# Layer 2's first norms and part products inside layer 1's last pair, and one pool for masked weights and parts

## The chip, the cores and the metric

The kernel runs on one core of one Trainium2 chip. The metric is the device time of one execution in microseconds (us); lower is better. A core has five engines that matter here: TensorE (PE), which multiplies matrices; VectorE (DVE); ScalarE (ACT); GpSimd (POOL); and SyncE (SP), which in this kernel only issues transfers. POOL issues transfers as well. Weights of a matmul are loaded into PE by an instruction of their own (PEld in the profile).

## The reference, cut to what matters

Four graph layers run one after another on `x` of shape (8, 2048, 64). Each adds its result to its input: normalise the 64 features, clip at zero, apply the layer, add. The change touches the seam between layer 1 and layer 2.

```python
# layer 1: attention over the neighbours
h = maximum(layernorm(x), 0)
h1 = h @ W
e = leaky_relu(s_src[:, :, None] + s_dst[:, None, :], 0.2)
attention = softmax(where(adj > 0.5, e, NEG_INF), axis=2)
x = x + elu(attention @ h1)

# layer 2: three steps of message passing, then layer 3
v = maximum(layernorm(x), 0)
v[:, 0] = intervention_value
for _ in range(3):
    effects = adj @ v
    h = relu(concat([v, effects]) @ W1.T + b1)
    v = h @ W2.T + b2
x = x + v
# layer 3: x, A x and 2 A (A x) - x, each with its own weights per node
```

## The kernel before, in words

The batch of 8 is handled as four pairs (`NP`). The two members of a pair lie one above the other in the 128 partitions, features by nodes, so a pair is a tile of 128 x 2048. It is worked on in four chunks of 512 nodes (`NCW`, `CW`). The adjacency stays on chip as sixteen tiles of 128 x 2048 (`aT` 0 to 11 and `aTl` for the last four).

**Layer 1** (`Layer1`, `run` at L1410) goes through the pairs. For a pair, `attend` (L1350) works on each half of the nodes: for each of sixteen tiles `m`, DVE makes two masked-weight tiles `pt` of 128 x 1024 (L1379), PE multiplies them with the features `hS` into `o` (`features`) and with `vd` into the denominator `dn` (`sums`). The order of the two alternates from tile to tile, so that the profile shows them as groups of two tiles. After each tile's first product, `between(m)` lets other work into the stream: the ends of the half before (`total`, whose product is `prd`, and `end`, which makes `res` and `e` and adds `e` to the pair's `x1` in memory by a POOL transfer), and a step of `neighbour_steps` (L1284). Those steps prepare the next pair: load `x`, norm it (`norm_steps`: `mean`, `xc`, square, `var`, logarithm and exponential, product), multiply with the weights (`ph`), and write the attention's row values to memory, from which `R` is loaded, one row repeated in all partitions. In the last pair there is no next pair and `between` only handles the ends.

**Layers 2 and 3** (`layers23`, L1474) begin when layer 1's pools are closed. `enter` (L1573) takes each chunk of the first pair through `normed` (L1542: the same norm) and `moved` (L1516): four products `py` with `W1e`, which are split into a high and a low part, `hi` by ACT (L1527) and `lo` by DVE (L1528). PE multiplies both parts with the adjacency, 16 tiles x 2 parts of 512 columns into `acc`. The first two chunks' input goes into `f_in`'s buffers, the other two into `room`, which shares its memory with the later `y1`. After the four `enter` chains the weights of layer 3 (`W3f`, `embf`) are loaded and two DVE operations (L1616, L1617) form combinations of them. Then come, for each pair, three steps of layer 2 and the products of layer 3. During the first two steps of each pair, raw adjacency chunks are loaded (`raw`, L1491) and checked on DVE (`check`, L1501).

The order of work on PE in both stages is that of the program (`kit.strict`, and `mm` at L713, whose line most matmuls carry). On the other engines a scheduler orders the instructions when the kernel is built. `Weave` interleaves the chains of layers 2 and 3 by the written delays. All pools have `reuse_waits="tile"`: a tile that takes over memory waits for the last user of the tile that lay there. Layer 1's pools are `l1_sb` and `l1_R` (right end of the on-chip memory), `att_pt` with 5 buffers for `pt`, and `att_sb`; layer 2 and 3 have `f_in`, `w2f` and `f_sb`, with 6 buffers each for `hi` and `lo`.

Of the kernel before, what the change touches and what calls it, by code (L numbers as in the profile page):

```python
# [16 lines left out]
P = 128  # L17
# [4 lines left out]
CW = 512  # L22
# [599 lines left out]
class Kit:  # L622
# [88 lines left out]
    def mm(self, *args, **kw):  # L711

        one = self.nc.tensor.matmul(*args, **kw)  # L713
        if self.strict:
            self.tc.keep_in_program_order(one)
# [10 lines left out]
    def norm_steps(self, dst, src, mean, var, xc, q):  # L726

        nc, mm = self.nc, self.mm
        n = dst.shape[-1] // CW
        for c in range(n):  # L730
            mm(mean[:, cols(c)], self.avg, src[:, cols(c)], start=True, stop=True)
        nc.vector.tensor_sub(xc, src, mean)
        nc.scalar.activation(q, xc, AF.Square)
        yield
        for c in range(n):
            mm(var[:, cols(c)], self.avg, q[:, cols(c)], start=True, stop=True)
        nc.scalar.activation(q, var, AF.Ln, bias=self.eps)
        nc.scalar.activation(q, q, AF.Exp, scale=-0.5)
        nc.vector.scalar_tensor_tensor(dst, xc, 0.0, q, op0=OP.max, op1=OP.mult)
        yield  # L740
# [525 lines left out]
class Layer1:  # L1266
# [6 lines left out]
    def __init__(self, kit, x1_dram):  # L1273
        tc, nc, t = kit.tc, kit.nc, kit.t
        self.kit, self.x1_dram = kit, x1_dram
        self.turn = 0
        self.l1 = l1 = ExitStack()
        dram = l1.enter_context(tc.tile_pool(name="r_dram", bufs=1, space=DRAM))
        self.r_dram = dram.tile([NP, 2, N], FP, name="r_dram")
        self.sb = sb = l1.enter_context(tc.tile_pool(name="l1_sb", bufs=2, side="right", reuse_waits="tile"))  # L1280
        self.R = l1.enter_context(tc.tile_pool(name="l1_R", bufs=2, side="right", reuse_waits="tile"))
        self.ps = ps = l1.enter_context(tc.tile_pool(name="l1_ps", bufs=1, space=PSUM, reuse_waits="tile"))

    def neighbour_steps(self, p):  # L1284

# [1 line left out]
        kit, sb, ps, Wx = self.kit, self.sb, self.ps, self.kit.W1x  # L1287
        nc, mm = kit.nc, kit.mm
        x1_dram, r_dram = self.x1_dram, self.r_dram
        hS = (self.sb2 if p % 2 else sb).tile([P, NT, P], FP, tag="hS", name="hS", bufs=1)  # L1290
        vd = sb.tile([P, NT, 2], FP, tag="vd", name="vd")
        sc = sb.tile([P, NT, 4], FP, tag="sc", name="sc", bufs=1)
        wd = sb.tile([P, NT, 2], FP, tag="wd", name="wd")
        for c in range(NCW):
            x = sb.tile([P, CW], FP, tag="x", name="x1", bufs=1)
            nc.sync.dma_start(out=x, in_=x1_dram[p, :, cols(c)])
            mean = ps.tile([P, CW], FP, tag="ln", name="mean")
            var = ps.tile([P, CW], FP, tag="ln", name="var")
            xc = sb.tile([P, CW], FP, tag="xc", name="xc")
            q = sb.tile([P, CW], FP, tag="q", name="q", bufs=1)  # L1300
            hn = xc
            for _ in kit.norm_steps(hn, x, mean, var, xc, q):
                yield
            for g in range(2):
                if g:
# [13 lines left out]
            yield  # L1319
# [30 lines left out]
    def attend(self, aT, p, hS, vd, wd, hf, between):  # L1350
# [24 lines left out]
        for m in range(NT):  # L1375
# [8 lines left out]
            order[0](m, pts)  # L1384
            between(m)
            order[1](m, pts)
        ds = self.sb.tile([P, CW], FP, tag="xc", name="ds")
        nc.vector.tensor_scalar_max(ds, dn, 1e-30)
        den = sb.tile([P, HN], FP, tag="den", name="den", bufs=1)

# [16 lines left out]

        return [lambda: total(0), end]

    def run(self, aT, now):  # L1410


        kit, l1 = self.kit, self.l1
        tc, nc = kit.tc, kit.nc
        self.pt = l1.enter_context(tc.tile_pool(name="att_pt", bufs=5, reuse_waits="tile"))
        self.sb2 = sb = l1.enter_context(tc.tile_pool(name="att_sb", bufs=2, reuse_waits="tile"))
        self.ps2 = l1.enter_context(tc.tile_pool(name="att_ps", bufs=2, space=PSUM, reuse_waits="tile"))
        kit.use_ln_exp()
        kit.strict = True
        ends = []  # L1420
        for p in range(NP):
            steps = self.neighbour_steps(p + 1) if p + 1 < NP else iter(())
            after = []

            def between(m):
                if m % NT and ends:
                    ends.pop(0)()

                for _ in range((2, 0, 1, 0, 1)[m % 5] - (m % 20 == 0)):
                    after.append(next(steps, None))  # L1430

            for hf in range(2):
                ends = self.attend(aT, p, *now, hf, lambda m: between(hf * NT + m))
            after.extend(steps)
            now = next((r for r in after if r), None)
        for e in ends:
            e()
        kit.strict = False
        l1.close()

# [30 lines left out]
            self.step(c)  # L1471


def layers23(kit, aT, x2_dram, x3_dram, out):  # L1474

    tc, nc, t, mm = kit.tc, kit.nc, kit.t, kit.mm
    ctx = ExitStack()
    W1v, W1e, W2, Wvc, Wec, cb = kit.W1v, kit.W1e, kit.W2, kit.Wvc, kit.Wec, kit.cb
    b1, b2c, ivc, b1c = kit.b1, kit.b2c, kit.ivc, kit.b1c
    K3, D3 = 3, 16  # L1480
    LAST = NCW - 1

    fin = ctx.enter_context(tc.tile_pool(name="f_in", bufs=2, reuse_waits="tile"))
    w2 = ctx.enter_context(tc.tile_pool(name="w2f", bufs=1, reuse_waits="tile"))
    sb = ctx.enter_context(tc.tile_pool(name="f_sb", bufs=2, reuse_waits="tile"))
    ps = ctx.enter_context(tc.tile_pool(name="f_ps", bufs=2, space=PSUM, reuse_waits="tile"))
    weave = Weave()
    todo = [(m, h) for m in range(NT) for h in range(NCW)]
    v = fin.tile([P, N], FP, name="v", bufs=1)

    def raw(n):  # L1491

# [15 lines left out]

    def parts(lent):

        tags = (lent, lent) if lent else (("hi", 6), ("lo", 6))
        return [sb.tile([P, 4, P], FR, tag=g, name=n, bufs=k) for n, (g, k) in zip(("hi", "lo"), tags)]

    LENT = (None, None, ("fold", 2), ("pr", 3))

    def moved(v, c, W, bias, lent=None):  # L1516

        py = ps.tile([P, 4, P], FP, tag="tp", name="py")
        for k in range(4):
            m = 4 * c + k  # L1520
            mm(py[:, k, :], v[:, m * P : (m + 1) * P], W, start=True, stop=True)
        hi, lo = parts(lent)
        if bias is not None:
            yb = fin.tile([P, 4, P], FP, tag="ca", name="yb")
            nc.vector.tensor_tensor(yb, py, bias[:, None, :].to_broadcast([P, 4, P]), op=OP.add)  # L1525
            py = yb
        nc.scalar.copy(hi, py)  # L1527
        nc.vector.tensor_tensor(lo, py, hi.bitcast(FP), op=OP.subtract)  # L1528
        return hi, lo
# [40 lines left out]
    def chunk_of(src, c):  # L1570
        return load(fin.tile([P, CW], FP, tag="x", name="xp"), src, c)
# [29 lines left out]
        yn[c] = turned(y1, c)  # L1601

    kit.strict = True
    y = [None] * NCW
    room = sb.tile([P, N], FP, tag="y1", name="room", bufs=1)
    for c in range(NCW):
        xp = chunk_of(x2_dram[0], c) if c < 2 else load(room[:, cols(c)], x2_dram[0], c)
        weave.start(enter(c, y, xp, 2.0 * c, ("u0", "u1")))
    weave.until(lambda: not weave.chains)
    W3 = w2.tile([P, K3, D3 * F], FP, name="W3f")  # L1610
    for h in range(2):
        nc.sync.dma_start(out=W3[half(h)], in_=t["L3_gnn_weight"])
    emb = w2.tile([P, NT, D3], FP, name="embf")
    nc.sync.dma_start(out=emb, in_=t["L3_gnn_embedding"].rearrange("(t p) d -> p t d", p=P))

    nc.vector.tensor_sub(W3[:, 0, :], W3[:, 0, :], W3[:, 2, :])  # L1616
    nc.vector.tensor_scalar(W3[:, 2, :], W3[:, 2, :], 2.0, None, op0=OP.mult)  # L1617
    every = range(NT)
    for p in range(NP):
        for step in range(3):  # L1620
            yn = [None] * NCW
            for c in range(NCW):
                acc = ps.tile([P, CW], FP, tag="acc", name="acc")
                if step < 2:
# [89 lines left out]
def four_layers(  # L1714
# [13 lines left out]
    with ExitStack() as s:  # L1728
# [29 lines left out]
            return steps()  # L1758

        layer0(kit, hn, x1, early, late_tile, between)  # L1760
        ahead[0].run(aT, ahead[1])
        layers23(kit, aT, x1, x3, out)
        ps = s.enter_context(tc.tile_pool(name="flag_ps", bufs=1, space=PSUM))
        nc.vector.tensor_reduce(kit.bad[:, 0:1], kit.bad, AX.X, OP.add)
        pb = ps.tile([F, 1], FP, name="pbad")
# [46 lines left out]
```

## Time and profile before

| | us |
|---|---|
| median of 3 runs | 2111.59 (2110.44 to 2114.61) |
| the profiled execution | 2106.54 |
| its span, first to last instruction | 2104.7 |
| layer 1's first attention product | starts at 529.08 |
| layer 1's last attention product | ends at 938.98 |
| first `acc` product of layer 2 | starts at 970.56 |
| granted TensorE clock, mean | 0.983 |

A line of a group gives the line of the program, the engine, the operation, what is written and what is read, the shapes and the count. In the chain and in the lists in order of time, the first number is the start in us from the span's beginning and the second the length. A product of fp32 operands is recorded as two instructions. "issue" is time for which the profile shows no cause. The span is cut into windows where that is more telling than the whole.

### The profile page before, as it was taken

To read this page: it belongs to the slowest core of one execution; us is meant where nothing else is said; L and a number is where in the kernel's file an instruction comes from. 1 tells how busy PE (TensorE), PEld (TensorE's weight loads), DVE (VectorE), ACT (ScalarE), POOL (GpSimd) and SP (SyncE) were. 2 spreads that over 40 slices of the span, in tenths; PEclk is the share of its full clock that TensorE was granted. 3 is DMA by queue.
4 is the path that set the end of the run, shared out by engine and by line. 5 is a ranking of instruction groups with operands and counts; after the bars stand their busy time and mean duration, and the time that the engine had idled before them with its cause. 6 is when DMAs were issued, how large, how long until landed. Compare 5 with 4: busy or idle time off the path is not lost.

```text
span 2104.7 us, 23660 instructions
## 1 busy us (share of the span) xinstructions
PE 2018.4 (96%) x9164; PEld 1156.8 (55%) x9164; DVE 1212.0 (58%) x1906; ACT 461.8 (22%) x863; POOL 260.1 (12%) x384
## 2 busy tenths in 40 slices
PE   7999989978999999997999999999999999999997
PEld 4777655623223233225776557775477755577653
DVE  6676488867888989973224662216542246522355
ACT  4322144466112121012121111110111211112100
POOL 0211154411000000000001120002110012100022
PEclk9999899989999999998999999999999999999999
DMA  5666271154111111113210012201012001121000
GB/s 128 195 187 192 100 233 47 36 160 155 51 46 36 41 40 31 41 23 91 66 45 14 23 32 60 63 10 30 23 54 66 30 21 25 37 65 55 5 16 12
DMA packets 85001, 136.06 MB, mean 65 GB/s; under 512 B 32912, under 2 KB 33168, under 8 KB 82640
## 3 DMA queue, kind: packets, MB, share of 16 engines
q1 hardware_dynamic: 66832, 83.86, 13.6%
q0 software_dynamic: 18048, 50.60, 8.9%
q8 instruction: 74, 1.21, 0.2%
q14 instruction: 47, 0.39, 0.1%
HBM read 103.69 MB, written 30.74 MB: 64 GB/s over the span
## 4 chain that ended last, share of the span: by engine, by line
PE 67%; issue 15%; DVE 6%; POOL 5%; DMA 3%; ACT 2%; POOLq 0%; SPq 0%; DVEq 0%; ACTq 0%
PE acc L713 27%; PE o L713 11%; PE dn L713 6%; PE u L713 5%; PE acc L925 2%; PE pgs L1153 2%; PE var L713 2%; PE py L713 2%; PE mean L713 2%; POOL fold L1699 1%; DVE ex L1151 1%; POOL ot L1700 1%; PE ph L713 1%; POOL mix L1152 1%; DMA at<-in_adjT 1%
## 5 line engine op out<-in xcount | busy, mean ns | idle before, releaser
L713 PE MATMUL acc<-aT,hi 128*128 128x512 f32 x960 | 419.7, 437 | 0.0
L713 PE MATMUL acc<-aT,lo 128*128 128x512 f32 x960 | 379.6, 395 | 0.0
L1687 DVE TENSOR_TENSOR pr<-u,embf 128x512 f32<-128x512 f32 x256 | 170.7, 688 | 138.8 <-PE u L713 131.8
L1379 DVE SCALAR_TENSOR_TENSOR pt<-R,wd,aT 128x1024 f32<-128x1024 f32 x192 | 236.9, 1280 | 22.2 <-PE dn L713 9.4
L713 PE MATMUL o<-pt,hS 128*64 128x512 f32 x1024 | 238.9, 602 | 4.1 <-DVE pt L1379 4.1
L713 PE MATMUL u<-W3f,y 64*128 64x512 f32 x1024 | 241.0, 589 | 0.0
L713 PEld LDWEIGHTS acc<-aT,hi 128*128 128x128 f32 x960 | 180.6, 188 | 66.0 <-issue 29.2
L713 PEld LDWEIGHTS acc<-aT,lo 128*128 128x128 f32 x960 | 180.7, 188 | 56.8 <-issue 20.1
L713 PEld LDWEIGHTS u<-W3f,y 64*128 64x128 f32 x1024 | 99.2, 187 | 120.6 <-issue 120.6
L713 PEld LDWEIGHTS o<-pt,hS 128*64 128x64 f32 x1024 | 70.4, 137 | 164.0 <-issue 149.9
L713 PE MATMUL u<-W3f,v 64*128 64x512 f32 x512 | 138.8, 619 | 0.0
L925 PE MATMUL acc<-at,Y 128*128 128x512 f32 x512 | 134.8, 408 | 1.7 <-DVE ev L934 1.7
L713 PE MATMUL acc<-aTl,hi 128*128 128x512 f32 x320 | 131.2, 410 | 1.0 <-ACT hi L1538 1.0
L1525 DVE TENSOR_TENSOR yb<-py,cb_f 128x512 f32<-128x512 f32 x32 | 22.1, 692 | 190.4 <-PE py L713 190.4
L713 PE MATMUL acc<-aTl,lo 128*128 128x512 f32 x320 | 126.3, 395 | 1.1 <-DVE lo L1539 1.1
L713 PE MATMUL dn<-pt,vd 128*32 128x512 f32 x1024 | 125.2, 598 | 0.3 <-DVE pt L1379 0.3
L1699 POOL TENSOR_TENSOR fold<-fold 128x256 f32<-128x256 f32 x64 | 47.7, 745 | 548.2 <-DVE fold L1698 510.3
L925 PEld LDWEIGHTS acc<-at,Y 128*128 128x128 f32 x512 | 94.3, 192 | 24.6 <-issue 4.1
L1691 DVE TENSOR_TENSOR pr<-pr 128x512 f32<-128x512 f32 x128 | 88.1, 688 | 2.2
L1379 DVE SCALAR_TENSOR_TENSOR pt<-R,wd,aTl 128x1024 f32<-128x1024 f32 x64 | 80.0, 1282 | 10.3 <-PE dn L713 7.4
L1539 DVE TENSOR_TENSOR lo<-tp,hi 128x512 fp32r<-128x512 f32 x32 | 22.1, 692 | 107.1 <-ACT hi L1538 107.1
L1153 PE MATMUL pgs<-mix,S 128*128 128x512 f32 x128 | 69.8, 635 | 12.9 <-POOL mix L1152 12.3
(294 smaller groups left out, 2614.7 us busy)
## 6 DMA issues: line engine op xcount, KB each, us to landing
at<-in_adjT POOLq DMA_DIRECT2D x32, 512.0 KB, 4.6
raw<-in_adjT SPq DMA_DIRECT2D x64, 256.0 KB, 3.3
aT<-in_adjT POOLq DMA_DIRECT2D x12, 1024.0 KB, 5.3
xp<-xd SPq DMA_DIRECT2D x43, 256.0 KB, 2.9
R<-r_dram SPq DMA_DIRECT2D x14, 512.0 KB, 3.6
hi_dram<-hi SPq DMA_DIRECT2D x16, 264.0 KB, 2.5
lo_dram<-lo SPq DMA_DIRECT2D x16, 264.0 KB, 3.6
hhi<-hi_dram POOLq DMA_DIRECT2D x16, 264.0 KB, 3.1
```

The source lines that it names most:

```text
L713: one = self.nc.tensor.matmul(*args, **kw)
L925: mm(acc[p], Y[h][:, m, p, :], at[:, k, :], start=m + h == 0, stop=m == NT - 1 and h == 1)
L1151: nc.vector.scalar_tensor_tensor(ex, mix, 1.0, ex, op0=OP.max, op1=OP.min)
L1152: nc.gpsimd.tensor_tensor(mix, ex, wt[:, k, :, None].to_broadcast([P, B, F]), op=OP.mult)
L1153: return lambda: mm(flat(pg), S[:, k, :], flat(mix), start=k == 0, stop=k == NB - 1)
L1379: nc.vector.scalar_tensor_tensor(pt, R[b2], wd[:, m, b2 : b2 + 1], aT[m][:, s].bitcast(FP), op0=OP.max, op1=OP.mult)
L1525: nc.vector.tensor_tensor(yb, py, bias[:, None, :].to_broadcast([P, 4, P]), op=OP.add)
L1539: nc.vector.tensor_tensor(lo, tp, hi.bitcast(FP), op=OP.subtract)
L1687: nc.vector.tensor_tensor(a, u[h], emb[:, i, 8 * w : 8 * w + 8, None].to_broadcast([P, 8, F]), op=OP.mult)
L1691: nc.vector.tensor_add(pr[h], pr[h], a)
L1699: nc.gpsimd.tensor_add(fold[:, :, 0:2, :], fold[:, :, 0:2, :], fold[:, :, 2:4, :])
L1700: nc.gpsimd.tensor_add(ot, fold[:, :, 0, :], fold[:, :, 1, :])
```

## The change

The norms and part products of layer 2's first pair are issued as steps inside the last pair of layer 1, in place of the preparation of a next pair. A new class `Layers23` opens `f_in` at that point, on the right end, after layer 1's near pools are closed; its `front` yields twelve steps. Eight of them, the halves of four norms, are taken at the tiles in `LATE` (counted over both halves, 0 to 31). Two of the `py` steps come at tile 31, the other two behind the last tile and the first `total`; the last `end` follows. `room` is gone: the third and fourth chunk's input take turns in `f_in`'s two buffers.

The parts no longer have pools for `hi` and `lo`. One tile that holds both has the size of a `pt`, and both kinds take turns in one pool of six buffers, `att_pt`, which stays open through layers 2 and 3. The weights of layer 3 are loaded at the first pair's second step and combined at its third.

In layer 1, `l1_R` is opened ahead of `l1_sb`; both are closed before the last pair, whose `R` tiles come from a new pool `l1_late`. `vd` and `wd` of pairs 1 to 3 move to `att_sb`, `hS` is allocated after the first norm, and `ds` shares its memory with `res`.

```diff
@@ norm_steps
         for c in range(n):
+            if callable(var):
+                var = var()
             mm(var[:, cols(c)], self.avg, q[:, cols(c)], start=True, stop=True)
@@ Layer1.__init__
-        self.sb = sb = l1.enter_context(tc.tile_pool(name="l1_sb", bufs=2, side="right", reuse_waits="tile"))
-        self.R = l1.enter_context(tc.tile_pool(name="l1_R", bufs=2, side="right", reuse_waits="tile"))
+        self.near = near = ExitStack()
+        self.R = near.enter_context(tc.tile_pool(name="l1_R", bufs=2, side="right", reuse_waits="tile"))
+        self.sb = near.enter_context(tc.tile_pool(name="l1_sb", bufs=2, side="right", reuse_waits="tile"))
+        self.lasting = ExitStack()
@@ neighbour_steps
+        keep = self.sb2 if p else sb
+        vd = keep.tile([P, NT, 2], FP, tag="vd", name="vd", bufs=1 + (p > 0))
+        wd = keep.tile([P, NT, 2], FP, tag="wd", name="wd", bufs=1 + (p > 0))
...
+            if hS is None:
+                hS = (self.sb2 if p % 2 else sb).tile([P, NT, P], FP, tag="hS", name="hS", bufs=1)
@@ attend
-        ds = self.sb.tile([P, CW], FP, tag="xc", name="ds")
+        ds = sb.tile([P, CW], FP, tag="res", name="ds", bufs=1)
@@ Layer1.run
-        self.pt = l1.enter_context(tc.tile_pool(name="att_pt", bufs=5, reuse_waits="tile"))
+        self.pt = self.lasting.enter_context(tc.tile_pool(name="att_pt", bufs=6, reuse_waits="tile"))
...
-            steps = self.neighbour_steps(p + 1) if p + 1 < NP else iter(())
+            last = p == NP - 1
+            if last:
+                self.near.close()
+                self.R = l1.enter_context(tc.tile_pool(name="l1_late", bufs=2, reuse_waits="tile"))
+            steps = following(self.ps, self.pt, self.lasting) if last else self.neighbour_steps(p + 1)
...
-                for _ in range((2, 0, 1, 0, 1)[m % 5] - (m % 20 == 0)):
+                n = (m in LATE) + 2 * (m == 2 * NT - 1) if last else (2, 0, 1, 0, 1)[m % 5] - (m % 20 == 0)
+                for _ in range(n):
                     after.append(next(steps, None))
...
+            if last:
+                ends.pop(0)()
             after.extend(steps)
             now = next((r for r in after if r), None)
-        for e in ends:
-            e()
+        ends.pop()()
@@ layers 2 and 3
+LATE = (4, 7, 9, 12, 14, 17, 19, 22)
+
+class Layers23:
+    def parts(self):
+        both = self.part.tile([P, 2, 4, P], FR, tag="pt", name="parts")
+        return [both[:, h] for h in range(2)]
+
+    def front(self, ps):
+        kit, fin = self.kit, self.fin
+        nc = kit.nc
+        xs = {}
+        for c in range(2):
+            xs[c] = fin.tile([P, CW], FP, tag="x", name="xp")
+            nc.sync.dma_start(out=xs[c], in_=self.x2_dram[0, :, cols(c)])
+        ca = [fin.tile([P, CW], FP, tag="ca", name="xc") for c in range(2)]
+        self.v = v = fin.tile([P, N], FP, name="v", bufs=1)
+        for d in (0, 2):
+            two = []
+            for c in range(d, d + 2):
+                mean = ps.tile([P, CW], FP, tag="ln", name="mean")
+                var = lambda: ps.tile([P, CW], FP, tag="h", name="var")
+                xc = ca[c] if d == 0 else fin.tile([P, CW], FP, tag="ca", name="xc")
+                two.append(kit.norm_steps(v[:, cols(c)], xs.pop(c), mean, var, xc, v[:, cols(c)]))
+                next(two[-1])
+                if d == 0:
+                    xs[c + 2] = fin.tile([P, CW], FP, tag="x", name="xp")
+                    nc.sync.dma_start(out=xs[c + 2], in_=self.x2_dram[0, :, cols(c + 2)])
+                yield
+            for c in range(d, d + 2):
+                next(two[c - d])
+                if c == 0:
+                    nc.vector.tensor_copy(v[:, 0:1], kit.ivc)
+                yield
+        self.y = []
+        for c in range(NCW):
+            py = ps.tile([P, 4, P], FP, tag=("ln", "h")[c % 2], name="py")
+            for k in range(4):
+                m = 4 * c + k
+                kit.mm(py[:, k, :], v[:, m * P : (m + 1) * P], kit.W1e, start=True, stop=True)
+            hi, lo = self.parts()
+            nc.scalar.copy(hi, py)
+            nc.vector.tensor_tensor(lo, py, hi.bitcast(FP), op=OP.subtract)
+            self.y.append((hi, lo))
+            yield
...
-        tags = (lent, lent) if lent else (("hi", 6), ("lo", 6))
+        if lent:
+            return [sb.tile([P, 4, P], FR, tag=lent[0], name=n, bufs=lent[1]) for n in ("hi", "lo")]
+        return self.parts()
...
-    room = sb.tile([P, N], FP, tag="y1", name="room", bufs=1)
-    for c in range(NCW):
-        xp = chunk_of(x2_dram[0], c) if c < 2 else load(room[:, cols(c)], x2_dram[0], c)
-        weave.start(enter(c, y, xp, 2.0 * c, ("u0", "u1")))
-    weave.until(lambda: not weave.chains)
+    y = self.y
...
+    def weights(step):
+        if step == 1:
+            for h in range(2):
+                nc.sync.dma_start(out=W3[half(h)], in_=t["L3_gnn_weight"])
+            nc.sync.dma_start(out=emb, in_=t["L3_gnn_embedding"].rearrange("(t p) d -> p t d", p=P))
+            return
+        nc.vector.tensor_sub(W3[:, 0, :], W3[:, 0, :], W3[:, 2, :])
+        nc.vector.tensor_scalar(W3[:, 2, :], W3[:, 2, :], 2.0, None, op0=OP.mult)
...
+            if p == 0 and step:
+                weights(step)
```

More of the change, by code (lines that the diff above doesn't have):

```diff
@@ L1279, in __init__ @@
         self.r_dram = dram.tile([NP, 2, N], FP, name="r_dram")
-        self.sb = sb = l1.enter_context(tc.tile_pool(name="l1_sb", bufs=2, side="right", reuse_waits="tile"))
-        self.R = l1.enter_context(tc.tile_pool(name="l1_R", bufs=2, side="right", reuse_waits="tile"))
-        self.ps = ps = l1.enter_context(tc.tile_pool(name="l1_ps", bufs=1, space=PSUM, reuse_waits="tile"))
+        self.near = near = ExitStack()
+        self.R = near.enter_context(tc.tile_pool(name="l1_R", bufs=2, side="right", reuse_waits="tile"))
+        self.sb = near.enter_context(tc.tile_pool(name="l1_sb", bufs=2, side="right", reuse_waits="tile"))
+        self.lasting = ExitStack()
+        self.ps = l1.enter_context(tc.tile_pool(name="l1_ps", bufs=1, space=PSUM, reuse_waits="tile"))
     def neighbour_steps(self, p):
@@ L1289, in neighbour_steps @@
         x1_dram, r_dram = self.x1_dram, self.r_dram
-        hS = (self.sb2 if p % 2 else sb).tile([P, NT, P], FP, tag="hS", name="hS", bufs=1)
-        vd = sb.tile([P, NT, 2], FP, tag="vd", name="vd")
+        keep = self.sb2 if p else sb
         sc = sb.tile([P, NT, 4], FP, tag="sc", name="sc", bufs=1)
-        wd = sb.tile([P, NT, 2], FP, tag="wd", name="wd")
+        vd = keep.tile([P, NT, 2], FP, tag="vd", name="vd", bufs=1 + (p > 0))
+        wd = keep.tile([P, NT, 2], FP, tag="wd", name="wd", bufs=1 + (p > 0))
+        hS = None
         for c in range(NCW):
@@ L1408, in attend, with run @@
         return [lambda: total(0), end]
-    def run(self, aT, now):
+    def run(self, aT, now, following):
         kit, l1 = self.kit, self.l1
         tc, nc = kit.tc, kit.nc
-        self.pt = l1.enter_context(tc.tile_pool(name="att_pt", bufs=5, reuse_waits="tile"))
+        self.pt = self.lasting.enter_context(tc.tile_pool(name="att_pt", bufs=6, reuse_waits="tile"))
         self.sb2 = sb = l1.enter_context(tc.tile_pool(name="att_sb", bufs=2, reuse_waits="tile"))
@@ L1471, in until, with __init__, run @@
             self.step(c)
-def layers23(kit, aT, x2_dram, x3_dram, out):
+LATE = (4, 7, 9, 12, 14, 17, 19, 22)
+class Layers23:
+    def __init__(self, kit, x2_dram, x3_dram, out, part, ctx):
+        self.part = part
+        self.kit, self.x2_dram, self.x3_dram, self.out = kit, x2_dram, x3_dram, out
+        self.ctx = ctx
+        self.fin = self.ctx.enter_context(kit.tc.tile_pool(name="f_in", bufs=2, side="right", reuse_waits="tile"))
+    def parts(self):
[38 more added lines that the diff above has]
+            yield
+    def run(self, aT):
+        layers23(self, aT)
@@ L1476, in layers23 @@
+def layers23(self, aT):
+    kit, x2_dram, x3_dram, out, ctx, fin, v = (
+        self.kit, self.x2_dram, self.x3_dram, self.out, self.ctx, self.fin, self.v
+    )
     tc, nc, t, mm = kit.tc, kit.nc, kit.t, kit.mm
-    ctx = ExitStack()
     W1v, W1e, W2, Wvc, Wec, cb = kit.W1v, kit.W1e, kit.W2, kit.Wvc, kit.Wec, kit.cb
@@ L1481, in layers23 @@
     LAST = NCW - 1
-    fin = ctx.enter_context(tc.tile_pool(name="f_in", bufs=2, reuse_waits="tile"))
     w2 = ctx.enter_context(tc.tile_pool(name="w2f", bufs=1, reuse_waits="tile"))
@@ L1488, in layers23 @@
     todo = [(m, h) for m in range(NT) for h in range(NCW)]
-    v = fin.tile([P, N], FP, name="v", bufs=1)
     def raw(n):
@@ L1509, in parts @@
     def parts(lent):
-        tags = (lent, lent) if lent else (("hi", 6), ("lo", 6))
-        return [sb.tile([P, 4, P], FR, tag=g, name=n, bufs=k) for n, (g, k) in zip(("hi", "lo"), tags)]
+        if lent:
+            return [sb.tile([P, 4, P], FR, tag=lent[0], name=n, bufs=lent[1]) for n in ("hi", "lo")]
+        return self.parts()
     LENT = (None, None, ("fold", 2), ("pr", 3))
@@ L1521, in moved, with in_parts @@
             mm(py[:, k, :], v[:, m * P : (m + 1) * P], W, start=True, stop=True)
+        return in_parts(py, bias, lent)
+    def in_parts(py, bias=None, lent=None):
         hi, lo = parts(lent)
@@ L1603, in layers23 @@
     kit.strict = True
-    y = [None] * NCW
-    room = sb.tile([P, N], FP, tag="y1", name="room", bufs=1)
-    for c in range(NCW):
-        xp = chunk_of(x2_dram[0], c) if c < 2 else load(room[:, cols(c)], x2_dram[0], c)
-        weave.start(enter(c, y, xp, 2.0 * c, ("u0", "u1")))
-    weave.until(lambda: not weave.chains)
+    y = self.y
     W3 = w2.tile([P, K3, D3 * F], FP, name="W3f")
-    for h in range(2):
-        nc.sync.dma_start(out=W3[half(h)], in_=t["L3_gnn_weight"])
     emb = w2.tile([P, NT, D3], FP, name="embf")
-    nc.sync.dma_start(out=emb, in_=t["L3_gnn_embedding"].rearrange("(t p) d -> p t d", p=P))
-    nc.vector.tensor_sub(W3[:, 0, :], W3[:, 0, :], W3[:, 2, :])
-    nc.vector.tensor_scalar(W3[:, 2, :], W3[:, 2, :], 2.0, None, op0=OP.mult)
+    def weights(step):
[6 more added lines that the diff above has]
+        nc.vector.tensor_scalar(W3[:, 2, :], W3[:, 2, :], 2.0, None, op0=OP.mult)
     every = range(NT)
@@ L1760, in four_layers, with following @@
         layer0(kit, hn, x1, early, late_tile, between)
-        ahead[0].run(aT, ahead[1])
-        layers23(kit, aT, x1, x3, out)
+        later = []
+        def following(ps, part, ctx):
+            later.append(Layers23(kit, x1, x3, out, part, ctx))
+            return later[0].front(ps)
+        ahead[0].run(aT, ahead[1], following)
+        later[0].run(aT)
         ps = s.enter_context(tc.tile_pool(name="flag_ps", bufs=1, space=PSUM))
```

## The prediction

> **What bounds the kernel now.** I read the page first, then the chain of work around the end of layer 1, then busy time by windows, then TensorE (PE) alone in order of time. The page's first part:
>
> ```profile
> PE 2018.4 (96%) x9164; PEld 1156.8 (55%) x9164; DVE 1212.0 (58%) x1906; ACT 461.8 (22%) x863; POOL 260.1 (12%) x384
> ```
>
> PE is the only engine near its limit, so the change can only bring what it takes out of PE's own sequence: idle time there, or matmuls that run slower than elsewhere. The windows cover the two halves of layer 1's last pair and what follows up to the first matmul of layer 2's first step (columns: window, length, busy time of PE, weight load, VectorE (DVE), ScalarE (ACT), GpSimd (POOL), granted clock, DMA share, GB/s):
>
> ```profile
> 850.30:896.40 46.10, 46.10 (x264) 12.79 (x260) 42.30 (x37) 4.37 (x5) 0.83 (x1) 1.00 0.11 24
> 896.40:939.00 42.60, 42.60 (x241) 11.80 (x237) 35.79 (x30) 4.37 (x5) 0.84 (x1) 1.00 0.12 21
> 938.98:970.56 31.58, 17.99 (x54) 8.56 (x53) 11.38 (x16) 13.34 (x20) 0.84 (x1) 0.73 0.52 110
> ```
>
> The last pair keeps PE full at clock 1.00. The third window is the hole: 31.58 us, 13.6 of them idle, at 0.73 of the clock. The chain says what it is made of:
>
> ```profile
> 948.62 5.38 DMA xd<-e
> ...
> 955.52 10.27 DMA W3f<-in_L_gnn_weight
> ...
> 969.60 1.13 PE py L713 x8
> 970.72 9.65 PE acc L713 x38
> ```
>
> Attention's last result is written back, then loads and norms of layer 2 follow one after another. PE's own waits between 937 and 971 us:
>
> ```profile
> PE mean L713 <- DMA room<-xd: 8.5, 1, 8.5
> PE var L713 <- ACT v L1548: 2.9, 2, 2.5
> PE py L713 <- DVE v L1554: 1.4, 2, 1.2
> PE prd L713 <- ACT den L1394: 0.7, 1, 0.7
> ```
>
> That is 13.5 us, and all four go when the norms stand elsewhere. The matmuls that stay cost less there too: first rows of the second half, last row of the hole:
>
> ```profile
> 894.59 1.92 PE L713 MATMUL dn<-pt,vd 128*32 128x512 f32 x16
> 896.45 1.12 PE L713 MATMUL prd<-ds,wide 64*128 64x512 f32 x2
> 897.50 3.65 PE L713 MATMUL o<-pt,hS 128*64 128x512 f32 x16
> ...
> 957.31 2.05 PE L713 MATMUL mean<-room,avg_f 128*128 128x512 f32 x2 [8.55 <-DMA room<-xd]
> ```
>
> One 512-column product (two records) put into the attention stream delays what follows by 897.50 - 896.45 = 1.05 us; in the hole it takes up to 2.05.
>
> **Part 1: the hole.** From the end of the last products to the first `acc` matmul, 938.98 to 970.56, is 31.58 us. Afterwards the same place holds two denominator products (2 x 1.06 = 2.1) and four part products `py` (969.60 to 970.56 gives 0.96 each, 3.8): 5.9. Taken out: 25.7 us. This needs every operand in time. After the sums of tile 15 PE runs py, py, products, prd, py, py, prd, acc. The first py's hi and lo take 0.59 on ACT and 0.69 on DVE, and the third py needs them gone: the second py, the products (1.87) and prd lie between, 3.9 us. The last py's hi and lo (1.3 us) are needed at tile 12 of the first chain, 12 x 0.47 = 5.6 us after it starts. No wait there.
>
> **Part 2: what the last pair takes in.** Eight norm matmuls (mean and var of four chunks) at 1.06 each: +8.5 us of PE, in full, because PE there is full. Here a rule speaks otherwise. The Trainium skill, "Perfetto Trace Analysis", section Identifying the Most-Contended Engine, says that matmul busy time is no good measure of how close PE is to its limit and that weight-load busy time should be used. By that, PE is at 12.79 of 46.10 us, 28%, the norms would find room, and the sum would be -25.7. But the row above shows the next product starting 1.05 us later for one insertion. I take the row: 31.58 - 5.9 - 8.5 = 17.2 us gained.
> DVE gains four `xc` and four `v` at 0.69, 5.5 us (and two `lo` at the end), against 3.8 + 6.8 us idle in the two windows plus the 8.5 by which PE lengthens them; hidden. ACT gains four times 0.63 + 0.69 + 0.63 and two `hi`: 9.0 us beside 80 idle. Without cover on DVE each of the twelve steps would cost PE about 1.3 us (rival A).
>
> **Part 3: loads and queues.** Four x loads of 256 KB move to SP ahead of the second half's R loads. The first two wait for buffers of pair 2 that its last readers leave at about 847 us, land 2.9 us later, and are needed at tile 4, where PE comes at 861.5 (the rows of the profile: features of tile 4 end there): 11 us of margin. The third and fourth wait for `xc` of the first two chunks, about 863 and 872. Behind them on SP stand the R loads, the last of which is issued only at 887.35 now: margin 15 us. Behind the `mean` matmul stands all of PE, since its order is fixed, so a late x would cost 1:1. POOL issues the same write-back as before; nothing on the path waits for it any longer.
> W3 (2 x 768 KB) and the embedding move to step 1, ahead of two raw loads on SP. W3 takes 10.3 us to land; even if the raws wait for all of it, 1012.2 + 1.7 (issues) + 10.3 + 3.3 = 1027.5, and DVE, which stands at `check` from 1020.2, is next due at 1027.43 for a `yb` whose parts only the next step reads. Cost 0; without that cover, the last chunk's parts have about 4 us. The two W3 operations on DVE (1.13 + 0.68) fall into its 7.1 us idle before 1055: 0.
>
> **Part 4: six masked-weight buffers instead of five.** PE shows small stalls where products take 4.03, 3.98 or 4.15 us instead of 3.65, and twice 0.15: about 0.9 in each of pairs 1 and 2 and 1.0 in pair 3, 2.8 in all, always just after `res` and `e` on DVE. One more tile of lead is 1.2 us of DVE work. Between -2.8 (all gone) and +1 (the DVE order shifts for the worse; nothing excludes it) I take -1.3. The parts take the buffer six back, whose readers are two tiles old; hi and lo freed together instead of apart is one matmul, 0.23 us, where ACT waits for its data and not for a buffer: 0.
>
> **Part 5: unknowns.** The first `acc` may get the bank of the second half's `o`, which `res` frees about 3 us after the last prd: 0 to +3, taken as 0, because before, a `mean` ran at 941.84 while `res` began at 943.66. Layer 1's buffers lie elsewhere during layer 0's end: -2 to +2, taken as 0, since all their loads there are interleaved with slack.
>
> **Sum.** -25.7 + 8.5 - 1.3 = -18.5 us. The profiled execution took 2106.54 (span 2104.7), 5 below the median of the runs; I carry the difference over to the median: 2111.59 - 18.5 = 2093.1. The new span would be near 2086.
>
> **Rivals.**
> A. DVE becomes the bound in the last pair: `xc` waits for `mean` in DVE's order, its lead over PE is lost, and each norm step leaves PE waiting 1.0 to 1.5 us (0.69 + 1.28 minus the 0.93 of sums). Eight to twelve steps: +8 to +15, so 2101 to 2108. For it: DVE is at 42.3 of 46.1. Against: pair 2 has more such steps per tile and lost 0.9 us. 7%.
> B. Slower: the preparation of layer 1's first pair, which now runs beside layer 0's end, lands on memory that layer 0 still holds, because its pools are laid out anew. Its place in the chain now:
>
> ```profile
> 470.48 4.40 DMA x<-xd
> 474.88 0.14 issue
> 475.01 2.05 PE mean L713 x2
> ```
>
> If it could only start when layer 0 ends (528), four chunks of norms and products would stand alone. The same work took 34 us (936.38 to 970.56) in the hole. 2111.6 - 18.5 + 34 = 2127. It decides from about 18 us of delay: the first `mean` later than about 480 instead of 460. Against: that memory's stage was over well before 453. 4%.
> C. PE has room after all (the rule of part 2): -25.7 and more, 2084 to 2086. 5%.
> D. The change does not do what it says: x loads or buffers hold the steps back to the end of the pair, the hole only changes its contents: 2108 to 2112. 4%.
>
> **How the numbers follow.** The forecast has 80%, its own range 2088 to 2099. A measurement of this kernel can tell about 0.2% (4.2 us) from no change. Faster: forecast, A and C, 0.92. Same: D, 0.04. Slower: B, 0.04. The range 2086 to 2101 takes in the bounds of parts 4 and 5 and the near ends of A and C.
>
> **What would show it.** Right: between the last products and the first `acc` about 6 us without a PE wait; the last pair about 97 us instead of 88.7; `W3f` and `room` gone from the chain; granted clock 1.00 throughout; 3.65 us products after `res`. Wrong: PE waits on `pt` or on `x` in the last pair (A, D), a wait of `acc` on `res` (part 5), the first attention product later than 529 (B), a last pair of only 89 us (C).

## The result and the profile after

The changed kernel took 2094.63 us (median of 4 runs, 2090.09 to 2100.02) against 2113.1 for the kernel before in the same comparison: ratio 0.9913, 95% interval 0.9885 to 0.9941. In a second comparison with more runs (e9) it took 2092.82 against 2111.67, ratio 0.9909, interval 0.9893 to 0.9926. The forecast was 2093.1 with a range of 2086 to 2101.

The profiled execution took 2095.15 us, its span is 2093.3. Against the span before, 2104.7, that is only 11.4 less, while the medians differ by 18. The profile before was one of the quickest executions of that kernel; what the change did has to be read by stages. Three marks are enough: F, the first attention product of layer 1; P, the first `prd` in the last pair's stream (it belongs to the end of pair 2 and stands behind the last pair's first two tiles); A, the first `acc` product of layer 2. Where the end of a group of matmuls is used as a mark, it is the start of the next group, since groups overlap a little in the profile.

| | F | F to P | P to A | F to A | A to the span's end |
|---|---|---|---|---|---|
| before | 529.08 | 321.27 | 120.21 | 441.48 | 1134.14 |
| changed | 534.27 | 322.90 | 102.16 | 425.06 | 1133.97 |

From F on the change brings 16.4 us; behind A nothing moved. Before F, where nothing was meant to change, the profile of the changed kernel is 5.2 us later. The medians differ by 18.5 and 18.9, some 2 us more than the marks show; that is within the first comparison's interval (12.5 to 24.3 us) and the second's (15.6 to 22.6).

The page's first part shows the same PE work in a shorter span:

```profile
PE 2017.3 (96%) x9164; PEld 1153.1 (55%) x9164; DVE 1211.8 (58%) x1906; ACT 461.6 (22%) x863; POOL 260.1 (12%) x384
```

The last pair by windows (window, length, busy time of PE, weight load, DVE, ACT, POOL, granted clock, DMA share, GB/s), first half, second half, and what was the hole:

```profile
857.17:908.06 50.89, 50.89 (x274) 13.88 (x270) 44.55 (x42) 8.89 (x12) 0.83 (x1) 1.00 0.15 37
908.06:951.40 43.34, 43.34 (x239) 11.82 (x235) 35.83 (x31) 7.29 (x10) 0.85 (x1) 1.00 0.10 19
951.40:959.33 7.93, 7.93 (x48) 4.79 (x44) 3.09 (x5) 2.94 (x5) 0.00 (x0) 1.00 0.00 0
```

The hole is closed: PE is busy in all of the last window and at full clock. PE in order of time shows the order written in the program, the four parts around the last products:

```profile
951.40 2.05 PE L713 MATMUL py<-W1e_f,v 128*128 128x128 f32 x16
953.38 1.94 PE L713 MATMUL o<-pt,hS 128*64 128x512 f32 x8
955.25 1.12 PE L713 MATMUL prd<-ds,wide 64*128 64x512 f32 x2
956.30 2.05 PE L713 MATMUL py<-W1e_f,v 128*128 128x128 f32 x16
958.28 1.12 PE L713 MATMUL prd<-ds,wide 64*128 64x512 f32 x2
959.33 1.12 PE L713 MATMUL acc<-v,W1v_f 128*128 128x512 f32 x2
```

From the last products' end (955.25) to `acc` it is 4.08 us, with the two `py` ahead of them (953.38 - 951.40 = 1.98) 6.06. But a new loss stands at the start of the last pair:

```profile
846.37 1.94 PE L713 MATMUL o<-pt,hS 128*64 128x512 f32 x8
849.51 1.07 PE L713 MATMUL o<-pt,hS 128*64 128x512 f32 x2 [1.20 <-DVE pt L1387]
851.82 3.54 PE L713 MATMUL o<-pt,hS 128*64 128x512 f32 x6 [1.24 <-DVE pt L1387]
855.29 1.95 PE L713 MATMUL dn<-pt,vd 128*32 128x512 f32 x16
```

Two tiles' products usually take 3.58 us from start to the next group's start; here 855.29 - 846.37 = 8.92, so 5.3 are lost, more than the 1.20 and 1.24 in brackets. DVE and SP at the same place say why:

```profile
840.20 2.48 DVE L1387 SCALAR_TENSOR_TENSOR pt<-R,wd,aTl 128x1024 f32<-128x1024 f32 x2 [0.25 <-PE dn L713]
846.51 0.69 DVE L1396 TENSOR_SCALAR ds<-dn 128x512 f32<-128x512 f32 x1 [3.83 <-PE dn L713]
848.17 1.28 DVE L1387 SCALAR_TENSOR_TENSOR pt<-R,wd,aT 128x1024 f32<-128x1024 f32 x1 [0.97 <-DMA R<-r_dram]
850.48 8.46 DVE L1387 SCALAR_TENSOR_TENSOR pt<-R,wd,aT 128x1024 f32<-128x1024 f32 x7 [1.03 <-DMA R<-r_dram]
```

```profile
823.25 0.32 SPq L1337 DMA_DIRECT2D r_dram<-rr  x1
842.71 1.29 SPq L1355 DMA_DIRECT2D R<-r_dram  x3
```

In the kernel before:

```profile
825.02 62.64 SPq L1347 DMA_DIRECT2D R<-r_dram  x4
```

The write to `r_dram` is issued at 823.25, but the `R` loads of the last pair leave SP only at 842.71, three at once. Before, the first left at 825.02. In SP's instruction order the first of the three is an `R` of the pair's *second* half, which takes the memory of an `R` of pair 2 and so waits for the last masked-weight tile of that pair (840.20 + 2.48 = 842.68 on DVE). The two `R` that the first half needs stand behind it on the same queue.

### The profile page after: what moved, and what is told of

It reads as the page before. It is cut to its first block, busy times and chain, and to the rows that moved or that the text cites. A ratio compares the mean times of both kernels' runs of the same rounds, so it can differ in the third digit from the quotient of the medians.

```text
span 2093.3 us, 23652 instructions
## 1 busy us (share of the span) xinstructions
PE 2017.3 (96%) x9164; PEld 1153.1 (55%) x9164; DVE 1211.8 (58%) x1906; ACT 461.6 (22%) x863; POOL 260.1 (12%) x384
## 4 chain that ended last, share of the span: by engine, by line
PE 68%; issue 15%; DVE 6%; POOL 5%; DMA 3%; ACT 2%; POOLq 0%; SPq 0%; DVEq 0%; ACTq 0%
PE acc L713 27%; PE o L713 11%; PE dn L713 6%; PE u L713 6%; PE acc L927 2%; PE pgs L1155 2%; PE var L713 2%; PE mean L713 2%; PE py L713 2%; POOL fold L1780 1%; DVE ex L1153 1%; PE ph L713 1%; POOL ot L1781 1%; DMA at<-in_adjT 1%; POOL mix L1154 1%
## 5 line engine op out<-in xcount | busy, mean ns | idle before, releaser
L713 PE MATMUL acc<-aT,parts 128*128 128x512 f32 x1664 | 456.0, 420 | 0.0
L713 PEld LDWEIGHTS acc<-aT,parts 128*128 128x128 f32 x1664 | 307.8, 188 | 111.8 <-issue 49.4
L713 PE MATMUL acc<-aTl,parts 128*128 128x512 f32 x384 | 103.1, 405 | 0.0
L713 PEld LDWEIGHTS acc<-aTl,parts 128*128 128x128 f32 x384 | 72.2, 188 | 21.5 <-issue 5.7
L1754 ACT COPY xs<-px 128x128 f32<-128x128 f32 x64 | 17.1, 267 | 272.7 <-POOL ot L1782 210.2
L1154 POOL TENSOR_TENSOR mix<-ex,wt 128x512 f32<-128x512 f32 x64 | 66.6, 1042 | 74.1 <-DVE ex L1153 65.0
L1672 POOL TENSOR_TENSOR bq<-bq,xp 128x512 f32<-128x512 f32 x16 | 20.5, 1282 | 434.1 <-DVE xp L1670 395.6
```

The costliest lines, as they stand in the source:

```text
L1154: nc.gpsimd.tensor_tensor(mix, ex, wt[:, k, :, None].to_broadcast([P, B, F]), op=OP.mult)
L1672: nc.gpsimd.tensor_add(bq, bq, xp)
```

## The experiments

The marks are those above. Ratios are to the kernel before, with their 95% intervals. The versions of the changed kernel lie so close together that their medians hardly tell them apart; what tells is the distance between two marks.

### e1: the last pair's R loads in the program's order

```diff
-        self.kit.nc.sync.dma_start(out=r, in_=self.r_dram[...])
+        one = self.kit.nc.sync.dma_start(out=r, in_=self.r_dram[...])
+        if p == NP - 1:
+            self.kit.tc.keep_in_program_order(one)
```

> The four R loads of the last pair are held to the program's order on SP; in the changed kernel the scheduler put the first R load of the last pair's second half ahead of the two that its first half needs. Theory: this order alone is what makes PE wait 1.20 and 1.24 us at the start of the last pair; with the program's order the waits go, and from the first attention product to the last pair's first prd it is 320.5 us instead of 322.9 (median 2092 against 2094.6). Rival: the loads wait because the new pool for R lies on memory that pair 2 still reads; then 322.9 stays.

2092.81 us, ratio to before 0.9901 (0.9887 to 0.9915). F to P is 858.76 - 539.70 = 319.06 us, against 322.90; F to A 421.21. So the order on SP was most of the loss, not the memory of the new pool: with the same pool the two loads of the first half now leave at 831.55.

```profile
831.55 0.81 SPq L1355 DMA_DIRECT2D R<-r_dram  x2
```

It is not all of it. PE still has one long group, and DVE stands at `ds` although `R` is there (PE first, then DVE):

```profile
851.77 5.21 PE L713 MATMUL o<-pt,hS 128*64 128x512 f32 x16
856.90 1.92 PE L713 MATMUL dn<-pt,vd 128*32 128x512 f32 x16
```

```profile
851.91 0.69 DVE L1398 TENSOR_SCALAR ds<-dn 128x512 f32<-128x512 f32 x1 [3.83 <-PE dn L713]
852.52 12.04 DVE L1389 SCALAR_TENSOR_TENSOR pt<-R,wd,aT 128x1024 f32<-128x1024 f32 x10
```

`ds` needs PE's last sums of pair 2. It stands ahead of the next pair's tiles in DVE's order, so DVE is idle for 3.83 us while PE finishes, and then PE waits for the tiles.

### e2: six buffers in the kernel before

```diff
-        self.pt = l1.enter_context(tc.tile_pool(name="att_pt", bufs=5, reuse_waits="tile"))
+        self.pt = l1.enter_context(tc.tile_pool(name="att_pt", bufs=6, reuse_waits="tile"))
```

> The kernel before with six buffers for the masked weights instead of five, nothing else. Theory: the small stalls after res and e (0.9 in pairs 1 and 2, 1.0 in pair 3) are DVE's lead running out; a sixth buffer takes about half of them or more: from the first attention product to the end of the last one 408 instead of 409.9 us, time 0.999 of before. Rival: the lead is set by DVE's order, not by buffers: 409.9 stays.

2105.3 us, ratio 0.996 (0.9948 to 0.9971): faster by 7, where 2 were expected. F to P fell from 321.27 to 317.40, P to the last product's end from 88.63 to 87.64, 4.9 us in all. That is a little under the interval of the times (6.1 to 11.0 us); where the rest would lie, the profile doesn't show. DVE's lead over PE runs out indeed, but the expectation had sized the loss wrongly. PE before, in pair 1:

```profile
647.24 4.03 PE L713 MATMUL o<-pt,hS 128*64 128x512 f32 x16
651.20 0.72 PE L713 MATMUL ph<-W1x,xc 128*128 128x132 f32 x4
651.85 1.90 PE L713 MATMUL dn<-pt,vd 128*32 128x512 f32 x10
653.90 1.06 PE L713 MATMUL dn<-pt,vd 128*32 128x512 f32 x6 [0.15 <-DVE pt L1379]
654.89 0.72 PE L713 MATMUL ph<-W1x,xc 128*128 128x132 f32 x4
```

The bracket says 0.15, but sixteen sums that take 1.85 from start to start took 654.89 - 651.85 = 3.04. With 0.38 and 0.33 in the `o` groups that is 1.9 in this pair, and pair 2 repeats it. With six buffers the same place reads

```profile
654.91 3.65 PE L713 MATMUL o<-pt,hS 128*64 128x512 f32 x16
658.50 0.72 PE L713 MATMUL ph<-W1x,xc 128*128 128x132 f32 x4
659.15 1.92 PE L713 MATMUL dn<-pt,vd 128*32 128x512 f32 x16
661.00 0.72 PE L713 MATMUL ph<-W1x,xc 128*128 128x132 f32 x4
```

and nothing is lost. So by the marks the sixth buffer, which the parts share, is by itself worth more than a quarter of the whole gain.

### e3: all twelve steps behind the last pair

```diff
-                n = (m in LATE) + 2 * (m == 2 * NT - 1) if last else (2, 0, 1, 0, 1)[m % 5] - (m % 20 == 0)
+                n = 0 if last else (2, 0, 1, 0, 1)[m % 5] - (m % 20 == 0)
```

> The changed kernel with all twelve steps behind the last tile of layer 1, as the loads, pools and the late W3 stay as changed. Theory (the place in PE's stream is what pays): the last pair shrinks by 8.5 us and the stretch from its last product to the first acc grows from 4 to 20 to 25 us, most of it PE idle; time 8 to 12 us above the changed kernel, 2103 to 2107. Rival (the gain came from the early x loads and from moving W3 and room out of the way): the stretch stays near 12 us and the time near 2095.

2098.32 us, ratio 0.9933 (0.9918 to 0.9949): less of a loss than the theory said, more than the rival said. From the last product's end (941.61) to A (960.55) it is 18.94 us, just under the 20 to 25 expected; F to A is 429.54, only 4.5 more than in the changed kernel. PE's waits in that stretch:

```profile
PE var L713 <- ACT v L739: 2.3, 2, 1.2
PE mean L713 <- DVE xc L732: 1.6, 2, 0.8
PE py L713 <- DVE parts L1543: 0.8, 1, 0.8
```

4.7 us of idle, not most of the stretch, is all that was left to hide. The last pair without the norms takes 941.61 - 853.97 = 87.64 us, with them 96.10: inside the pair they cost PE 8.5 us, about what they cost behind it. The place in the stream is worth the idle time and no more. The other 12.6 us of the hole (31.58 - 18.94) went with all PE work still behind the pair. Only the first two x loads are early here (845.21); the other two leave SP at 944.54 and 946.45, and yet no wait of PE is put down to a load. e6 shows what `room` alone is worth.

### e4: the norm products twice

```diff
-            mm(mean[:, cols(c)], self.avg, src[:, cols(c)], start=True, stop=True)
+            for _ in range(1 + self.twice):
+                mm(mean[:, cols(c)], self.avg, src[:, cols(c)], start=True, stop=True)
```

(the same for `var`; `twice` is set when `Layers23` begins)

> The changed kernel with each of the eight mean and var products of the first pair's norms issued twice into the same place (the second replaces the first). Theory (PE is full in the last pair): each extra product costs its 1.05 us, 8.5 us in all, 2103; the last pair from its first prd to its last product grows by 8.5 us. Rival (PE has room there, as weight-load busy time says): 0 to 2 us.

2101.99 us, ratio 0.9948 (0.9929 to 0.9968). From P to the first `py` it is 959.38 - 858.29 = 101.09 us against 94.23, 6.9 more for eight products. One row shows the size:

```profile
869.42 1.98 PE L713 MATMUL mean<-xp,avg_f 128*128 128x512 f32 x4
871.33 1.92 PE L713 MATMUL dn<-pt,vd 128*32 128x512 f32 x16
```

Two products move the next group by 1.91, one by 1.06 (868.30 to 869.36 in the changed kernel): the second costs 0.85. PE is full there, and work put in is paid for. Rival C of the prediction, with the weight-load share as its reason, is out.

### e5: R and ds held in order

```diff
@@ as e1, and
-        ds = sb.tile([P, CW], FP, tag="res", name="ds", bufs=1)
-        nc.vector.tensor_scalar_max(ds, dn, 1e-30)
+        got = []
...
         def total(k):
+            if not got:
+                got.append(sb.tile([P, CW], FP, tag="res", name="ds", bufs=1))
+                one = nc.vector.tensor_scalar_max(got[0], dn, 1e-30)
+                if p == NP - 2 and hf:
+                    kit.tc.keep_in_program_order(one)
+            ds = got[0]
```

> As e1, and the denominator's maximum ds of pair 2's second half held on DVE behind the first four masked-weight tiles of the last pair (in e1 DVE still stood 3.83 us at ds, which waits for PE's last sums, with R loaded; PE then waited 1.6 us). Theory: the rest of the last pair's late start is this order on DVE; from the first attention product to the last pair's first prd 317.4 us as in e2 (319.1 in e1, 322.9 in the changed kernel), no product of 5.21 us; 2090 to 2092. Rival: DVE cannot be earlier because the R tiles land late; 319 stays.

2089.66 us, ratio 0.9896 (0.988 to 0.9913): the lowest median of all versions, though its interval overlaps that of the changed kernel. `ds` is issued inside `total` in all halves here, and held to that place for pair 2's second half. F to P is 855.10 - 537.32 = 317.78, F to A 419.93, 5.1 less than in the changed kernel. The start of the last pair is regular:

```profile
844.22 3.65 PE L713 MATMUL o<-pt,hS 128*64 128x512 f32 x16
847.80 1.92 PE L713 MATMUL dn<-pt,vd 128*32 128x512 f32 x16
849.66 3.65 PE L713 MATMUL o<-pt,hS 128*64 128x512 f32 x16
853.24 1.92 PE L713 MATMUL dn<-pt,vd 128*32 128x512 f32 x16
855.10 1.12 PE L713 MATMUL prd<-ds,wide 64*128 64x512 f32 x2
```

The loss of 5.5 us (322.90 against 317.40 in e2) was thus, but for 0.4, two orders that the scheduler chose: `R` on SP (3.8 by e1) and `ds` on DVE (1.3 more).

### e6: the kernel before without room

```diff
-    room = sb.tile([P, N], FP, tag="y1", name="room", bufs=1)
+    W3 = w2.tile([P, K3, D3 * F], FP, name="W3f")
     for c in range(NCW):
-        xp = chunk_of(x2_dram[0], c) if c < 2 else load(room[:, cols(c)], x2_dram[0], c)
+        xp = chunk_of(x2_dram[0], c) if c < 2 else load(W3[:, 0, cols(c - 2)], x2_dram[0], c)
```

> The kernel before, with the third and fourth chunk's x loaded into W3f's memory instead of room, so that these loads don't wait for the write-back of e; W3 is loaded after them. Norms and parts stay behind layer 1. Theory: room's wait (8.55 us) and the half-speed products behind it go: the stretch from the last attention product to the first acc falls from 31.6 to 20 to 23 us, time 2101 to 2104, that is more than half of what the change brought, without any work moved into the last pair. Rival: the next late thing (W3 on DVE, ahead of the last lo) takes its place and 27 us or more stay, 2108.

2103.85 us, ratio 0.9966 (0.9956 to 0.9976). The time is as the theory said, the stretch lies between the two expectations: it falls from 31.58 to 24.95 us, by 6.6 us. That is about 40% of the change's gain, where the theory had said more than half. The wait of 8.5 on the load becomes

```profile
PE var L713 <- ACT v L1548: 4.2, 2, 3.8
PE mean L713 <- DMA W3f<-xd: 1.6, 1, 1.6
```

Before, the loads left SP as in the first line; here they leave as in the second:

```profile
954.14 0.80 SPq L1567 DMA_DIRECT2D room<-xd  x2
946.55 0.90 SPq L1567 DMA_DIRECT2D W3f<-xd  x2
```

So `room`'s wait was real and was due to its memory: `room` took over what `e` still held, and could be loaded only when `e` was written back (948.62 + 5.38 = 954.00 in the chain before). What stays is mainly the wait for the squares on ACT, not W3. W3 is combined at 967.68, after A (963.99), and PE doesn't wait for it.

From here to e3 it is another 6.0 us (24.95 - 18.94). The windows of the two stretches, e6 first, then e3:

```profile
939.04:963.99 24.95, 17.33 (x54) 8.34 (x53) 9.84 (x14) 13.35 (x20) 0.84 (x1) 0.79 0.55 123
941.61:960.55 18.94, 14.23 (x54) 7.09 (x53) 7.80 (x13) 10.39 (x17) 0.00 (x0) 1.00 0.19 56
```

With the same number of recorded matmuls, PE is busy for 3.1 us less at a granted clock of 1.00 instead of 0.79, and idle for 2.9 less. In e6 ACT works first on `e` of the last attention result and comes to the norm's squares 8.0 us behind the last product (947.03 - 939.04); PE's longest wait there is 3.81. In e3 that end is issued behind the parts, the squares start 2.9 us behind the last product (944.55 - 941.61), and the longest wait is 1.16. No run moved the last end alone, so this share of it is read from the traces, not shown by an experiment.

### e7: W3 ahead of step 0

```diff
+    weights(1)
+    weights(2)
     every = range(NT)
...
-            if p == 0 and step:
-                weights(step)
```

> The changed kernel with the load and the two combinations of W3 ahead of layer 2's first step, where they stood before. Theory: DVE waits for W3 for up to 10 us in its order, but only check and yb stand behind, whose results the next step reads; from the first attention product to the end of the span within 1 us of the changed kernel (1559.0), time 2093 to 2097. Rival: the parts of the first chunks come late and PE waits: 3 to 8 us more.

2092.45 us, ratio 0.9921 (0.9899 to 0.9943), the same as the changed kernel. DVE waits for W3 and PE does not notice:

```profile
973.24 1.23 DVE L1694 TENSOR_TENSOR W3f<-W3f 128x1024 f32<-128x1024 f32 x1 [4.67 <-DMA W3f<-in_L_gnn_weight]
```

From A to the end it is 1133.75 us against 1133.97. F to P was 320.15, 2.7 shorter than in the changed kernel: the `R` loads leave SP late in the same way (842.05), but the slowest lands after 5.3 us instead of 6.7, and DVE waits for `R` once instead of twice. Why that load was quicker stays open. Moving W3 was worth nothing in this kernel, although the chain before names its transfer with 10.27 us.

### e8: the steps packed

```diff
-LATE = (4, 7, 9, 12, 14, 17, 19, 22)
+LATE = (4, 5, 6, 7, 8, 9, 10, 11)
```

> The changed kernel with the eight norm steps at eight tiles in a row (4 to 11) instead of spread over 4 to 22. Theory: DVE has the room in the last pair (a step adds 1.05 us to PE and 0.69 to DVE), so nothing changes: the last pair from its first prd to its first py stays at 94.2 us within 1.5, time 2093 to 2097. Rival (A of the prediction, DVE's lead runs out): 1.0 to 1.5 us a step, 8 us more.

2093.48 us, ratio 0.9921 (0.9906 to 0.9935). From P to the first `py`: 949.30 - 855.08 = 94.22, against 94.23. DVE has room even for eight norm steps in a row; rival A is out, and the careful spreading is not what makes it work.

### e9: the changed kernel again

> The changed kernel once more, as the reference of e1, e5, e7 and e8. The first attention product started anywhere from 529.1 to 539.7 us in the profiles so far, also where layer 0 is untouched. Theory: this start is chance and the rest repeats: from the first attention product to the first acc 425.1 within 1 us, median 2092 to 2096, about 4 us above e5. Rival: the late start of the changed kernel's first profile (534.3) belongs to the change: again 534 or later, and a rest that differs by as much.

2092.82 us. F to A is 959.78 - 534.73 = 425.05, within 0.01 of the first profile. F was 534.73, as late as the first time, so this run doesn't tell chance from the change. The other profiles say more: with layer 0 as before, F was 529.08, 529.13 (e6) and 536.91 (e2); with layer 0 as changed, 531.01 (e3) to 539.70 (e1). Both groups hold early and late ones, so a late F doesn't need the change. Nor would a lasting 5.2 us fit the times: it would leave a gain of 11.2, below both intervals (from 12.5 and from 15.6).

## Why the prediction was right

The total was right within 2 us, and the main mechanism too: the hole's waits went, and PE paid in full for the norms. That the total was so close is luck in part. One term of the sum was mis-sized and one was missing, and they nearly cancel; the marks then give 16.4 us, and the medians' 18.5 meets the forecast's 18.5 only within the scatter of the times.

| term | predicted | measured | by |
|---|---|---|---|
| hole closed | -25.7 | -25.5 (31.58 to 6.06) | trace |
| norms in the last pair | +8.5 | +8.45 | trace, e2, e3 |
| sixth buffer | -1.3 | -4.9 | e2 |
| R loads and ds out of order | not in the sum | +5.5 | trace against e2; 5.1 of it by e5 |
| sum from F to A | -18.5 | -16.4 | trace |

The norms' 8.45 comes from the last pair, which lost 1.0 of stalls and yet grew from 88.63 to 98.08 - 1.98 = 96.10 us. The span near 2086 did not come, it is 2093.3: 2.1 us are the sum's, 5.2 the later F.

**Part 1** held: no operand was late, `acc` didn't wait for `res`, and from P to A PE ran through at clock 1.00.

**Part 2** held, by the row and not by the rule: the Trainium skill ("Perfetto Trace Analysis", Identifying the Most-Contended Engine) judges PE's headroom by weight-load busy time and by the share of peak arithmetic. The first of the two, taken alone, would have made the norms free; the second was not worked out here. The last pair showed weight loads busy for 13.88 of 50.89 us and still paid for each product, once more in e4. The measurement decides: in this stage a low weight-load share is no room.

**Part 3** held for x, on which PE did not wait in the last pair, and for W3 and the raw loads, since A to the end is unchanged (e7 too). It failed in what it left out: it listed the x loads that go ahead of the second half's `R`, but not that the `R` loads themselves can change places on SP. That e1 could hold them in order shows that they could. One load with a late operand then held back two whose data had been issued at 823.25, until 842.71: a cost that the sum put at nothing.

**Part 4** had the mechanism, and its bound of -2.8 was too near. I counted stalls from the lengths of `o` groups and the brackets, and overlooked that a `dn` group was cut in two, 3.04 us from start to start instead of 1.85.

**Part 5**: `acc` had its bank free, taken as 0 rightly. For layer 0's end nothing points to the change, though a small delay could hide in the scatter of the times.

**The rivals.** A is out by e8, C by e4. B foresaw a delay from 18 us up and a slower kernel; F stays within 11 us of before, and the kernel is faster. D did not happen: the x loads were early. Two of the prediction's signs of being wrong did appear, for other reasons: PE waited on `pt` at the last pair's start (e1 and e5 give the cause), and F was later than 529. None of the rivals named where the gain really sits. The prediction let it look as if moving the work into the pair brought 17.2 us. By e3, 12.6 of them come with all norms still behind the pair: 6.6 from `room`'s memory (e6), 6.0 from the order behind the pair and the full clock there (read from the traces of e3 and e6). The move itself brings 4.5, the idle time that remained.

## What to carry to other kernels

Moving work into a stage where the same engine is full saved only the idle time around it, 4.5 us. First ask what the work waits for where it stands: memory still held by a write-back was worth 6.6 us here, and no work had to be moved for that. Read stalls from starts, from one group to the next, not from bracketed waits or lengths: 0.15 in brackets was 1.19 here, and 2.44 was 5.3. When a change lets a scheduler reorder a queue, look at each in-order queue for a transfer or operation with a late operand in front of one that is needed early.

## What was not expected of the hardware

A second product of the same shape and weights right behind the first costs 0.85 us where the first costs 1.06 (e4). What the 0.2 are for, no run shows.

The time before F varies by 8 to 9 us between programs whose layer 0 is the same, and part of it goes with PE's clock. Behind a wait for the same load, the two products `pf` take 1.05 us in the profiles of before and e3 and 2.00 in those of the changed kernel and of e2; of the kernel before, then of the changed one:

```profile
478.63 1.05 PE pf L1204 x2
481.21 2.00 PE pf L1206 x2
```

From 460 to 500 us the granted clock was 0.91 before and in e3, 0.83 in the changed kernel and 0.79 in e2. A difference of a few us between two single profiles is therefore no evidence for a change in the stages behind; the distance from F to A repeated to 0.01 us in two profiles of the changed kernel.
